# Sorting the second group's neighbour lists with one-hot matrix products inside layer 0, instead of through DRAM before it

## The chip, the core and the metric

The kernel runs on one core of a Trainium2 chip. The metric is the device time of one execution in microseconds (us). It ran three times before the change: 966.85, 970.43 and 974.26 us, so the median is 970.43 us. One further execution was profiled: it took 971.21 us, and its span from the first to the last instruction is 969.5 us.

## What is computed

The input is x with 3327 rows of 512 numbers, and a symmetric 0/1 matrix `adj` with about nine ones in a row. Two layers follow each other, each with a residual and a layer norm:

```
x = layernorm(x + relu(attention0(x, adj)))     # 4 heads of 128: softmax over the neighbours
x = layernorm(x + sigmoid(attn_a * x_a + attn_b * x_b))
    # x_a = weighted mean of h = x @ W_sa over the neighbours, x_b = adj @ (x @ W_g) + b
    # attn_a, attn_b = sigmoid of a sum over the neighbours of a scalar column
```

## The kernel before

The kernel is sparse. Row numbers are padded to 26 tiles of 128 nodes. It has three stages.

**Stage one (up to about 215 us).** For chunk after chunk of 512 nodes the adjacency is read, TensorE turns it into codes (line 379), and VectorE (DVE) extracts each node's neighbour numbers with repeated top-8 operations. The list of a node is a row of 32 words in `st`: its own number, 24 neighbour slots (S), its index in its group, and four words with its part of the attention logits. The nodes are in two groups, tiles 0 to 11 and tiles 12 to 25 (`NG`). Inside a group they are sorted by degree, so that a tile needs only as many slots as `CAPS` says. `rank_a` and `rank_b` (lines 454 to 485) give every node its place in the sorted order, `ranki`. `sort` (line 496) then moves the lists: one scatter per tile of 128 rows (helper at line 145) into the DRAM tensor `lists`, and one load (line 500) of the sorted lists into `srt`. For group 0 these steps are spread over stage one, between the stores of the feature rows to `table0` (line 361). For group 1 the rank is known only when the last chunk is decoded.

**Layer 0 (about 215 to 560 us).** Its loop (line 828) takes the 26 tiles in the hand-written order `order0`: tiles 11, 10, 0, 1, ..., 9 of group 0, then tile 23, tile 12 and the rest of group 1. Tiles 0 and 12 (`T0`) hold the nodes of the highest degree; their last slots are packed in a "staircase" that `climb` (line 542) prepares. In each iteration i, in program order:

- `gather` (line 592) for the tile three positions ahead (`AHEAD`): one indirect DMA per neighbour slot, issued by GpSimd (POOL), lines 609, 615 and 624, into a pool of seven buffers (`GB`) of six rows each;
- `publish` (line 793) of up to four finished tiles, after every fourth norm: ScalarE (ACT) scales them (line 795), and they are stored to `table1`;
- `columns2` (line 782): ACT copies the transposed rows of tile i-2 (line 784), TensorE (PE) multiplies them with eight columns (line 787);
- `attend` (line 748): for each slot DVE (line 760) or, for every third slot, ACT (line 758) weights the gathered row, and PE adds it up in PSUM with an identity product (bias at line 752, slots at line 763);
- for tile i-1: residual (line 843), transposes on PE (line 780), statistics, and at each fourth tile the inverse root (lines 669 to 676);
- `columns3` (line 790), in iteration 5 `climb(1)`, and `weigh_a`/`weigh_b` (lines 711, 738) of tile i+1: the logits (line 717), the exponential on ACT (line 730), and copies of the gathered node numbers into `srt` on ACT (line 734).

Each engine executes its instructions in the order in which they are written here; no scheduler reorders them.

The calls around the change stand ahead of the loop: the gathers of the first three tiles, then `sort(1)` with its 14 scatters on POOL and its load on SyncE's queue (SP), then two copies on SP (lines 811, 812) that build `own1`, a table of each group 1 node's x row beside its `table0` row. Group 1's gathers, from iteration 9 on, read `srt[1]` and `own1`.

**Layer 1 (about 560 us to the end).** The same gathers from `table1`, sums on DVE and PE, and two projections.

Of the kernel before, what the change touches and what calls it, by code (L numbers as in the profile page):

```python
# [8 lines left out]
F32 = mybir.dt.float32  # L9
AF = mybir.ActivationFunctionType  # L10
ALU = mybir.AluOpType
# [3 lines left out]
P = 128  # L15
LN_EPS = 1e-5
I32 = mybir.dt.int32
# [6 lines left out]
NG = (12, 14)  # L24
S = 24
# [4 lines left out]
LW = 32  # L30
# [49 lines left out]
def sparse_pass(  # L80
# [56 lines left out]
    dram = ctx.enter_context(tc.tile_pool(name="dram", bufs=1, space=bass.MemoryType.DRAM))  # L137
    table0 = dram.tile([NP, ROW], F32, name="table0")
    table1 = dram.tile([NP, ROW], F32, name="table1")
    own1 = dram.tile([NG[1] * P, 2, ROW], F32, name="own1")  # L140
    lists = [dram.tile([n * P, LW], I32, name=f"lists{i}") for i, n in enumerate(NG)]

    def scatter(group, dst, rows, src, last=None):

        put = nc.gpsimd.indirect_dma_start(  # L145
            out=dst, out_offset=bass.IndirectOffsetOnAxis(ap=rows, axis=0), in_=src, in_offset=None,
            bounds_check=last, oob_is_err=last is None,
        ).ins
# [8 lines left out]
    srt = [const.tile([P, n, LW], I32, name=f"srt{i}") for i, n in enumerate(NG)]  # L157
# [31 lines left out]
        return S + 1 if j in T0 else CAPS[j] + 1  # L189


    p0 = tc.alloc_tile_pool(name="p0", bufs=1, side="right")
    psl = tc.alloc_tile_pool(name="psl", bufs=1, space=PSUM, side="right")
    pj = tc.alloc_tile_pool(name="pj", bufs=1, side="left")
# [59 lines left out]
    for s in range(4):  # L254
# [5 lines left out]
        blk, pattern=[[P, 2]], base=0, channel_multiplier=1, allow_small_or_imprecise_dtypes=True  # L260
# [11 lines left out]
    )  # L272
    all1 = p0.tile([P, ND * NM], F32, name="all1")
    nc.gpsimd.memset(all1, 1.0)
    st = p0.tile([P, NT, LW], I32, name="st")
    nc.gpsimd.memset(st, 0)
    nc.gpsimd.iota(st[:, :, 0], pattern=[[P, NT]], base=0, channel_multiplier=1)
    for g, n in enumerate(NG):
        nc.gpsimd.iota(st[:, T0[g] : T0[g] + n, S + 1], pattern=[[P, n]], base=0, channel_multiplier=1)

    for s in range(2):
        for hh in range(2):
# [61 lines left out]
    def features(t):  # L344

        i = t * P // CH
        xc = xcs[i]
        o = t * P - chunks[i]
        pf = psf.tile([P, 2, 512], F32, tag="pf", name=f"pf{t}")
        for k, hh in ((k, hh) for hh in range(2) for k in range(KT)):  # L350
            nc.tensor.matmul(  # L351
                pf[:, hh, :HC], xc[:, k, o : o + P], w0[:, k, hh, :], start=(k == 0), stop=(k == KT - 1)
            )
        row = pj.tile([P, ROW], F32, tag="row", name=f"row{t}", bufs=4)
        nc.scalar.copy(row[:, 0:F].rearrange("p (h o) -> p h o", h=2), pf[:, :, 0 : F // 2])
        nc.scalar.activation(
            row[:, F : F + H], pf[:, 0, F // 2 : HC], AF.Identity, bias=pad if t == NT - 1 else 0.0
        )
        nc.scalar.copy(row[:, F + H : ROW], st[:, t, 0:1].to_broadcast([P, H]))
        nc.scalar.copy(st[:, t, S + 2 : S + 2 + H].bitcast(F32), pf[:, 1, F // 2 : HC])  # L360
        nc.gpsimd.dma_start(table0[t * P : (t + 1) * P, :], row)  # L361

    widths = [32 * ((len(ms) + 3) // 4) for ms in halves]
# [63 lines left out]
    def pick(i):  # L427

        t0, nt, g, l0 = span(i)
        nc.vector.tensor_reduce(ovf[:, t0 : t0 + nt, 0], codes_left[i][:, :nt], AX.X, ALU.max)  # L430
        nc.vector.tensor_scalar(ovf[:, t0 : t0 + nt, 1], ents[i][:, :nt, S - 1], -255.0, None, ALU.add)
        key = p0.tile([P, 4, S], F32, tag="key", name=f"key{i}")
        for j in range(nt):
            top8(nc, p0, key[:, j, :], cands[i][:, j].rearrange("p l s -> p (l s)"), LEVELS * S, "c", t0 + j)
        nc.vector.tensor_scalar(ovf[:, t0 : t0 + nt, 2], key[:, :nt, S - 1], -255.0, None, ALU.add)
        some = p0.tile([P, 4, S], F32, tag="some", name=f"some{i}")
        nc.vector.tensor_scalar(some[:, :nt], key[:, :nt], 255.5, None, ALU.is_gt)
        nc.vector.tensor_reduce(deg[g][:, l0 : l0 + nt], some[:, :nt], AX.X, ALU.add)
# [11 lines left out]
        nc.vector.tensor_scalar(st[:, t0 : t0 + nt, 1 : S + 1], some[:, :nt], float(N), None, ALU.add)  # L450

    hot = {}

# [10 lines left out]
    def rank_b(g):  # L464

        n = NG[g]
        w = ND * n
        oh = hot[g]
        tot = psl.tile([P, CH], F32, tag="pc0", name=f"tot{g}")
        nc.tensor.matmul(tot[:, :w], ones, oh, start=True, stop=True)  # L470
        pre = psl.tile([P, CH], F32, tag="pc1", name=f"pre{g}")
        nc.tensor.matmul(pre[:, :w], before, oh, start=True, stop=True)
        tots = p0.tile([P, ND * NM], F32, tag="tots", name=f"tots{g}")[:, :w]
        nc.vector.tensor_copy(tots, tot[:, :w])
        cum = p0.tile([P, ND * NM], F32, tag="cum", name=f"cum{g}")[:, :w]
# [9 lines left out]
        return ranki  # L485

    ranks = {}

# [2 lines left out]
    def later(n):  # L491
        for task in tasks[:n]:
            task()
        del tasks[:n]

    def sort(g, ranki, queue):

        put = lambda t: scatter(f"lists{g}", lists[g][:, :], ranki[:, t : t + 1], st[:, T0[g] + t, :])
        tasks.extend(lambda t=t: put(t) for t in range(NG[g]))
        tasks.append(lambda: queue.dma_start(srt[g], lists[g].rearrange("(t p) w -> p t w", p=P)))  # L500
        if g == 0:
            tasks.extend(lambda j=j: own_x(j) for j in range(NG[0]))
# [56 lines left out]
    for i in range(len(chunks)):  # L559
        make_codes(i)  # L560
        more(1)
        if i == NC0:
            rankis[0] = rank_b(0)
            sort(0, rankis[0], nc.gpsimd)
# [14 lines left out]
        more(4)  # L579
# [6 lines left out]


    gp = ctx.enter_context(tc.tile_pool(name="gp", bufs=1))
    m0 = ctx.enter_context(tc.tile_pool(name="m0", bufs=2))
    ps = ctx.enter_context(tc.tile_pool(name="ps", bufs=1, space=PSUM))  # L590

    def gather(table, j):
# [213 lines left out]
    AHEAD = 3  # L806
    for i in range(AHEAD):
        got[order0[i]] = gather(table0, order0[i])
    sort(1, rankis[1], nc.sync)
    later(len(tasks))  # L810
    nc.sync.dma_start(own1[:, 0, :], xo)
    nc.sync.dma_start(own1[:, 1, :], table0[NG[0] * P : NP, :])
    psl.release()
# [14 lines left out]
    for i in range(NT + 3):  # L828
# [21 lines left out]
                ]  # L850
        if 2 <= i < NT + 2:
            columns3(order0[i - 2])
        if i == 5:
            climb(1, m0, psx.tile([P, B * H], F32, tag="pcol", name="climb1", bufs=2)[:, : B + H])
        if i == NG[0]:
            nc.vector.memset(over, 0.0)
# [7 lines left out]
            weigh_b(order0[i + 1])  # L864
    covered()
    psx.release()


    w1 = ctx.enter_context(tc.tile_pool(name="w1", bufs=1, side="right"))
# [647 lines left out]
```

## Time and profile before

| | |
|---|---|
| runs | 966.85, 970.43, 974.26 us; median 970.43 |
| profiled execution | 971.21 us, span 969.5 us, mean granted TensorE clock 0.907 |
| busy | PE 804.4 us (83%), DVE 716.6 (74%), POOL 626.2 (65%), ACT 278.2 (29%) |
| chain that ended last | PE 45%, DVE 19%, DMA 12%, POOL 11%, issue 7%, ACT 4% |
| 180 to 215 us | PE busy 10.0 of 35, DVE 29.75, POOL 26.6 |
| 237 to 290 us | PE busy 47.4 of 53, DVE 32.3, POOL 40.5 |
| 420 to 500 us | PE busy 75.6 of 80, DVE 55.9, POOL 60.3 |

In a timeline, a row gives the start, the duration, engine, line and operation, output<-input and the count of instructions; in brackets the engine's idle time before it and what ended it. A float32 product appears as two MATMUL instructions. A POOL indirect DMA is about 0.96 us of work with 0.30 us to the next one, so 76% is what POOL shows when it issues without a pause.

### The profile page before, as it was taken

The numbers are of one execution on the slowest core, as the hardware profiler recorded it, in microseconds if no ns is written. First come the engines' busy times: TensorE is split into PE (matmuls) and PEld (weight loads), VectorE is DVE, ScalarE is ACT, GpSimd is POOL, SyncE is SP. The second block draws the span as 40 slices with busy tenths as digits, with TensorE's granted clock in tenths as the row PEclk, the third lists the DMA queues.
The fourth block names the chain that finished last, engine by engine and source line by source line (L and its number), as shares of the span: only waits on it lengthen the run. The fifth ranks groups of instructions, "written<-read, shape, count | busy, mean of one in ns | idle before, by whom it ended". The sixth has DMA issues, their size and how long they took to land.

```text
span 969.5 us, 10086 instructions
## 1 busy us (share of the span) xinstructions
PE 804.4 (83%) x2534; PEld 421.7 (43%) x2534; DVE 716.6 (74%) x2118; ACT 278.2 (29%) x820; POOL 626.2 (65%) x664
## 2 busy tenths in 40 slices
PE   4399887338897998989979839998989989899893
PEld 3277675114344444444434514444434434344341
DVE  4277878886465676667756738799989989989873
ACT  1022211004234343435333403223222232232231
POOL 6611144777777777677777367777777777777411
PEclk9699998557898999989998958999989999999997
DMA  9799999972988787787777257776676776666400
GB/s 321 289 353 376 399 332 382 360 205 76 401 312 247 218 271 225 257 282 231 231 227 232 92 166 192 195 187 188 189 197 196 187 195 183 187 185 188 129 33 36
DMA packets 74242, 221.87 MB, mean 229 GB/s; under 512 B 14944, under 2 KB 19216, under 8 KB 73280
## 3 DMA queue, kind: packets, MB, share of 16 engines
q0 software_dynamic: 47008, 153.87, 53.7%
q1 hardware_dynamic: 24512, 65.17, 17.7%
q10 hardware_dynamic: 2656, 2.10, 0.7%
q8 instruction: 23, 0.38, 0.2%
q14 instruction: 43, 0.35, 0.1%
HBM read 200.01 MB, written 28.55 MB: 236 GB/s over the span
## 4 chain that ended last, share of the span: by engine, by line
PE 45%; DVE 19%; DMA 12%; POOL 11%; issue 7%; ACT 4%; DVEq 0%; ACTq 0%; POOLq 0%
PE acc L763 21%; PE pf L351 9%; POOL g L615 7%; DMA g<-table,srt 7%; DVE sw L967 7%; DMA at<-in_adjB 3%; PE po L1007 3%; PE pcol L787 3%; PE acc L988 3%; PE acc L752 3%; DVE g L969 2%; ACT xt L784 1%; DMA a_row<-in_a_self 1%; PE x1t L780 1%; POOL sprod L321 1%
## 5 line engine op out<-in xcount | busy, mean ns | idle before, releaser
L615 POOL DMA_INDIRECT g<-table,srt x464 | 479.2, 1033 | 147.9 <-issue 121.9
L763 PE MATMUL acc<-g,ident 128*128 128x512 f32 x504 | 230.8, 614 | 1.4 <-DVE g L760 1.4
L967 DVE SCALAR_TENSOR_TENSOR sw<-g,e,sw 128x512 f32<-128x512 f32 x226 | 169.3, 749 | 12.7 <-ACT sw L951 8.5
L763 PEld LDWEIGHTS acc<-g,ident 128*128 128x128 f32 x504 | 100.4, 199 | 132.1 <-issue 101.1
L988 PE MATMUL acc<-g,ident 128*128 128x512 f32 x262 | 128.6, 618 | 24.9 <-DVE g L969 14.7
L351 PE MATMUL pf<-w,xc 128*128 128x260 f32 x416 | 102.2, 408 | 13.3 <-DVE w L291 13.3
L760 DVE TENSOR_TENSOR g<-g,w 128x512 f32<-128x512 f32 x176 | 110.5, 695 | 0.6
L1007 PE MATMUL po<-wg,sT 128*128 128x512 f32 x208 | 98.0, 616 | 0.0
L351 PEld LDWEIGHTS pf<-w,xc 128*128 128x128 f32 x416 | 83.6, 204 | 29.2 <-DVE w L291 14.1
L1007 PE MATMUL po<-wsa,sT 128*128 128x512 f32 x208 | 95.2, 601 | 0.3 <-ACT sT L1000 0.3
L758 ACT ACTIVATE g<-g,w 128x128 f32<-128x128 f32 x304 | 91.6, 389 | 0.7 <-DVE w L743 0.7
L988 PEld LDWEIGHTS acc<-g,ident 128*128 128x128 f32 x262 | 49.1, 193 | 95.8 <-issue 44.7
L361 POOL DMA_DIRECT2D table<-row x26 | 14.4, 555 | 85.4 <-ACT st L360 85.4
L969 DVE TENSOR_TENSOR g<-g 128x512 f32<-128x512 f32 x95 | 65.7, 692 | 3.3
L1037 ACT ACTIVATE za<-za 128x512 f32<-128x512 f32 x26 | 16.4, 631 | 170.8 <-DVE za L1035 170.8
L1007 PEld LDWEIGHTS po<-wg,sT 128*128 128x128 f32 x208 | 41.4, 200 | 52.2 <-issue 52.0
L1007 PEld LDWEIGHTS po<-wsa,sT 128*128 128x128 f32 x208 | 40.2, 194 | 51.3 <-issue 48.9
L145 POOL DMA_INDIRECT out<-za,srt x26 | 29.1, 1118 | 50.1 <-ACT za L1052 44.0
L787 PE MATMUL pcol<-v,xt 128*128 128x8 f32 x208 | 32.4, 283 | 33.1 <-ACT xt L784 33.1
L379 PE MATMUL pc<-at,pow 128*32 128x512 bf16 (+1 forms) x182 | 24.3, 436 | 33.2 <-DMA at<-in_adjB 19.4
L787 PEld LDWEIGHTS pcol<-v,xt 128*128 128x128 f32 x208 | 30.0, 222 | 38.8 <-ACT xt L784 38.6
L717 DVE TENSOR_TENSOR w<-g,srt 128x20 f32<-128x20 f32 (+3 forms) x55 | 9.7, 184 | 48.2 <-DMA g<-table,srt 46.9
(236 smaller groups left out, 933.3 us busy)
## 6 DMA issues: line engine op xcount, KB each, us to landing
at<-in_adjB SPq DMA_DIRECT2D x78, 512.0 KB, 11.4
g<-table,srt POOLq DMA_INDIRECT x464, 3.8
table<-row POOLq DMA_DIRECT2D x26, 260.0 KB, 6.2
xc<-in_xB SPq DMA_DIRECT2D x6, 1024.0 KB, 7.1
own<-in_xo SPq DMA_DIRECT2D x1, 3640.0 KB, 23.5
own<-table SPq DMA_DIRECT2D x1, 3640.0 KB, 42.0
at<-in_adjL SPq DMA_DIRECT2D x13, 256.0 KB, 13.2
table<-x1a SPq DMA_DIRECT2D x12, 260.0 KB, 5.7
```

The costliest lines, as they stand in the source:

```text
L145: put = nc.gpsimd.indirect_dma_start(out=dst, out_offset=bass.IndirectOffsetOnAxis(ap=rows, axis=0), in_=src, in_offset=None, bounds_check ...
L351: nc.tensor.matmul(pf[:, hh, :HC], xc[:, k, o : o + P], w0[:, k, hh, :], start=(k == 0), stop=(k == KT - 1))
L615: nc.gpsimd.indirect_dma_start(out=buf[:, q - q0, :], out_offset=None, in_=table[:, :], in_offset=bass.IndirectOffsetOnAxis(ap=srt[g][:, i ...
L752: nc.tensor.matmul(acc, ident, bias0, start=True, stop=False)
L758: nc.scalar.activation(gv[:, h, :], gv[:, h, :], AF.Copy, scale=w[:, s, h : h + 1])
L760: nc.vector.tensor_tensor(gv, gv, w[:, s, :].rearrange("p (h o) -> p h o", o=1).to_broadcast([P, H, FO]), ALU.mult)
L763: nc.tensor.matmul(acc, ident, buf[:, o + s - s0, 0:F], start=False, stop=(s == CAPS[j] and j not in T0))
L787: nc.tensor.matmul(pcol, xt1[:, k, :], v1[:, k, :], start=(k == 0), stop=(k == KT - 1))
L967: nc.vector.scalar_tensor_tensor(sw, g[:, i, 0:F], e[:, s : s + 1], sw, ALU.mult, ALU.add)
L969: nc.vector.tensor_add(g[:, i, 0:F], g[:, i - 1, 0:F], g[:, i, 0:F])
L988: nc.tensor.matmul(plain[j], to, row, start=(not sums_of_two and i == 0), stop=(sums_of_two and i == len(rows) - 1),)
L1007: nc.tensor.matmul(proj[j], sT[:, k, :], wt[:, k, :], start=(half + k == 0), stop=(half + k == KT))
```

## The change

- The lists of group 0 stay as they were (`st0`, `lists0`, `sort0`). The lists of group 1 are kept in float32 in `st1`, rows of 30 words, in a pool `ls` of its own. A small float32 tile `ids_f` holds the node numbers that `features` writes to `table0`.
- `rank_b(1)` also splits the place into tile and row, as float32 (`to`): four small DVE operations.
- `sort1` takes the place of `sort(1)`. For each of the 14 source tiles, DVE writes two operands, `row_is` (128x128: does this node go to that row?) and `spread` (128x420: the node's list in the columns of its destination tile, zeros elsewhere), each in two buffers. PE multiplies them and adds all 14 products up in one PSUM tile. Two source tiles are done in each of the iterations 1 to 7 of layer 0, after `columns3` and ahead of `weigh_a`. In iteration 7 DVE then copies the result to `srt[1]` in two parts.
- `climb(1)` moves from iteration 5 to iteration 8.
- The 14 scatters on POOL and the load on SP are gone; the `own1` copies on SP directly follow the last loads of the adjacency.
- The pool `m0` is released at the end of layer 0.

```diff
-    st = p0.tile([P, NT, LW], I32, name="st")
-    nc.gpsimd.memset(st, 0)
-    nc.gpsimd.iota(st[:, :, 0], pattern=[[P, NT]], base=0, channel_multiplier=1)
-    for g, n in enumerate(NG):
-        nc.gpsimd.iota(st[:, T0[g] : T0[g] + n, S + 1], pattern=[[P, n]], base=0, channel_multiplier=1)
+    st0 = p0.tile([P, NG[0], LW], I32, name="st0")
+    nc.gpsimd.memset(st0, 0)
...
+    st1 = ls.tile([P, NG[1], W1], F32, name="st1")
...
+    nc.gpsimd.iota(ids_f, pattern=[[P, NT]], base=0, **count)
...
+    columns = ls.tile([P, P], F32, name="columns")
+    nc.gpsimd.iota(columns, pattern=[[1, P]], base=0, **count)
+    tiles_ = ls.tile([P, NG[1], 1], F32, name="tiles_")
+    nc.gpsimd.iota(tiles_[:, :, 0], pattern=[[1, NG[1]]], base=0, **count)
...
+        ti = p0.tile([P, NM], I32, name="ti")
+        nc.vector.tensor_scalar(ti[:, :n], ranki[:, :n], 7, None, ALU.logical_shift_right)
+        nc.vector.tensor_scalar(ranki[:, :n], ranki[:, :n], P - 1, None, ALU.bitwise_and)
+        to = ls.tile([P, 2, NM], F32, name="to")
+        nc.vector.tensor_copy(to[:, 0, :n], ti[:, :n])
+        nc.vector.tensor_copy(to[:, 1, :n], ranki[:, :n])
...
+    def sort1(to, t0, t1):
+        n = NG[1]
+        if t0 == 0:
+            in_place.append(ps.tile([P, KT * P], F32, tag="pt", name="sorted1")[:, : n * W1])
+        for t in range(t0, t1):
+            row_is = ls.tile([P, P], F32, tag="row_is", name=f"row_is{t}", bufs=2)
+            nc.vector.tensor_scalar(row_is, columns, to[:, 1, t : t + 1], None, ALU.is_equal)
+            spread = ls.tile([P, n, W1], F32, tag="spread", name=f"spread{t}", bufs=2)
+            nc.vector.scalar_tensor_tensor(
+                spread, tiles_.to_broadcast([P, n, W1]), to[:, 0, t : t + 1],
+                st1[:, t : t + 1, :].to_broadcast([P, n, W1]), ALU.is_equal, ALU.mult,
+            )
+            nc.tensor.matmul(
+                in_place[0], row_is, spread.rearrange("p t w -> p (t w)"), start=(t == 0), stop=(t == n - 1)
+            )
+        if t1 == n:
+            by_tile = in_place[0].rearrange("p (t w) -> p t w", t=n)
+            nc.vector.tensor_copy(srt[1][:, :, : S + 2], by_tile[:, :, : S + 2])
+            nc.vector.tensor_copy(srt[1][:, :, S + 2 : W1].bitcast(F32), by_tile[:, :, S + 2 :])
...
-    sort(1, rankis[1], nc.sync)
-    later(len(tasks))
...
-        if i == 5:
+        if 0 < i <= 7:
+            sort1(rankis[1], 2 * i - 2, 2 * i)
+        if i == 8:
             climb(1, m0, psx.tile([P, B * H], F32, tag="pcol", name="climb1", bufs=2)[:, : B + H])
...
     psx.release()
+    m0.release()
```

More of the change, by code (lines that the diff above doesn't have):

```diff
@@ L140, in sparse_pass @@
     own1 = dram.tile([NG[1] * P, 2, ROW], F32, name="own1")
-    lists = [dram.tile([n * P, LW], I32, name=f"lists{i}") for i, n in enumerate(NG)]
+    lists0 = dram.tile([NG[0] * P, LW], I32, name="lists0")
     def scatter(group, dst, rows, src, last=None):
@@ L189, in slots @@
         return S + 1 if j in T0 else CAPS[j] + 1
+    ls = ctx.enter_context(tc.tile_pool(name="ls", bufs=1, side="right"))
     p0 = tc.alloc_tile_pool(name="p0", bufs=1, side="right")
@@ L274, in sparse_pass, with st @@
     nc.gpsimd.memset(all1, 1.0)
-    st = p0.tile([P, NT, LW], I32, name="st")
-    nc.gpsimd.memset(st, 0)
-    nc.gpsimd.iota(st[:, :, 0], pattern=[[P, NT]], base=0, channel_multiplier=1)
-    for g, n in enumerate(NG):
-        nc.gpsimd.iota(st[:, T0[g] : T0[g] + n, S + 1], pattern=[[P, n]], base=0, channel_multiplier=1)
+    st0 = p0.tile([P, NG[0], LW], I32, name="st0")
+    nc.gpsimd.memset(st0, 0)
+    nc.gpsimd.iota(st0[:, :, 0], pattern=[[P, NG[0]]], base=0, channel_multiplier=1)
+    nc.gpsimd.iota(st0[:, :, S + 1], pattern=[[P, NG[0]]], base=0, channel_multiplier=1)
+    count = dict(channel_multiplier=1, allow_small_or_imprecise_dtypes=True)
+    W1 = S + 2 + H
+    st1 = ls.tile([P, NG[1], W1], F32, name="st1")
+    nc.gpsimd.iota(st1[:, :, 0], pattern=[[P, NG[1]]], base=NG[0] * P, **count)
+    nc.gpsimd.iota(st1[:, :, S + 1], pattern=[[P, NG[1]]], base=0, **count)
+    ids_f = p0.tile([P, NT], F32, name="ids_f")
+    nc.gpsimd.iota(ids_f, pattern=[[P, NT]], base=0, **count)
+    count["channel_multiplier"] = 0
+    columns = ls.tile([P, P], F32, name="columns")
+    nc.gpsimd.iota(columns, pattern=[[1, P]], base=0, **count)
+    tiles_ = ls.tile([P, NG[1], 1], F32, name="tiles_")
+    nc.gpsimd.iota(tiles_[:, :, 0], pattern=[[1, NG[1]]], base=0, **count)
+    def st(t):
+        return (st0[:, t, :], st0[:, t, S + 2 : S + 2 + H].bitcast(F32)) if t < NG[0] else (
+            st1[:, t - NG[0], :], st1[:, t - NG[0], S + 2 : S + 2 + H]
+        )
     for s in range(2):
@@ L358, in features @@
         )
-        nc.scalar.copy(row[:, F + H : ROW], st[:, t, 0:1].to_broadcast([P, H]))
-        nc.scalar.copy(st[:, t, S + 2 : S + 2 + H].bitcast(F32), pf[:, 1, F // 2 : HC])
+        nc.scalar.copy(row[:, F + H : ROW], ids_f[:, t : t + 1].to_broadcast([P, H]))
+        nc.scalar.copy(st(t)[1], pf[:, 1, F // 2 : HC])
         nc.gpsimd.dma_start(table0[t * P : (t + 1) * P, :], row)
@@ L449, in pick @@
         )
-        nc.vector.tensor_scalar(st[:, t0 : t0 + nt, 1 : S + 1], some[:, :nt], float(N), None, ALU.add)
+        nc.vector.tensor_scalar(
+            (st0, st1)[g][:, l0 : l0 + nt, 1 : S + 1], some[:, :nt], float(N), None, ALU.add
+        )
     hot = {}
@@ L484, in rank_b @@
         ranks[g] = rk
-        return ranki
+        if g == 0:
+            return ranki
+        ti = p0.tile([P, NM], I32, name="ti")
[4 more added lines that the diff above has]
+        nc.vector.tensor_copy(to[:, 1, :n], ranki[:, :n])
+        return to
     ranks = {}
@@ L494, in later, with sort0 @@
         del tasks[:n]
[L496 to L502, printed above, removed]
+    def sort0(ranki):
+        put = lambda t: scatter("lists0", lists0[:, :], ranki[:, t : t + 1], st(t)[0])
+        tasks.extend(lambda t=t: put(t) for t in range(NG[0]))
+        tasks.append(lambda: nc.gpsimd.dma_start(srt[0], lists0.rearrange("(t p) w -> p t w", p=P)))
+        tasks.extend(lambda j=j: own_x(j) for j in range(NG[0]))
+    in_place = []
+    def sort1(to, t0, t1):
[9 more added lines that the diff above has]
+                st1[:, t : t + 1, :].to_broadcast([P, n, W1]), ALU.is_equal, ALU.mult,
+            )
+            nc.tensor.matmul(
+                in_place[0], row_is, spread.rearrange("p t w -> p (t w)"), start=(t == 0), stop=(t == n - 1)
+            )
+        if t1 == n:
+            by_tile = in_place[0].rearrange("p (t w) -> p t w", t=n)
+            nc.vector.tensor_copy(srt[1][:, :, : S + 2], by_tile[:, :, : S + 2])
+            nc.vector.tensor_copy(srt[1][:, :, S + 2 : W1].bitcast(F32), by_tile[:, :, S + 2 :])
     def own_x(j):
@@ L563, in sparse_pass @@
             rankis[0] = rank_b(0)
-            sort(0, rankis[0], nc.gpsimd)
+            sort0(rankis[0])
         turn_codes(i)
@@ L588, in sparse_pass @@
     gp = ctx.enter_context(tc.tile_pool(name="gp", bufs=1))
-    m0 = ctx.enter_context(tc.tile_pool(name="m0", bufs=2))
+    m0 = tc.alloc_tile_pool(name="m0", bufs=2, side="left")
     ps = ctx.enter_context(tc.tile_pool(name="ps", bufs=1, space=PSUM))
```

## The prediction, made before the changed kernel was run

> **What bounds the kernel now.** I read the 40 slices and the granted clock first, then the windows by stage, the chain of waits from 200 to 420 us, and the timelines of POOL, PE, DVE, ACT and SP there. The chain is mostly PE in layer 0 (acc L763 alone has 21% of the span). POOL shows where the change bites:
>
> ```profile
> 216.25 1.00 POOL L145 DMA_INDIRECT lists<-st,ranki  x1 [0.30 <-DVE w L729]
> ...
> 235.26 0.99 POOL L615 DMA_INDIRECT g<-table,srt  x1 [0.30 <-issue]
> ...
> 250.96 0.95 POOL L615 DMA_INDIRECT g<-table,srt  x1 [0.31 <-issue]
> ...
> 395.15 0.95 POOL L615 DMA_INDIRECT g<-table,srt  x1 [4.25 <-PE acc L763]
> ```
>
> The 14 scatters hold POOL from 216.25 to 235.26, 19.0 us. Behind them stand the 13 gathers of tile 1 (the loop's fourth); the last starts at 250.96 and lands at 257.25. POOL then issues without a pause until 390.9, where it waits 4.25 us for a buffer that layer 0's thirteenth iteration frees. So its 19 us of lag are worked off by then, and what the end feels of them is only the time that PE stood idle:
>
> ```profile
> 254.27 0.60 PE L780 MATMUL x1t<-ident,x1a 128*128 128x128 f32 x4
> 259.58 1.88 PE L787 MATMUL pcol<-v,xt 128*128 128x8 f32 x8 [4.71 <-ACT xt L784]
> 261.31 2.05 PE L752 MATMUL acc<-bias,ident 128*128 128x512 f32 x2
> 263.15 12.74 PE L763 MATMUL acc<-g,ident 128*128 128x512 f32 x26
> 275.73 0.60 PE L780 MATMUL x1t<-ident,x1a 128*128 128x128 f32 x4
> 277.06 1.06 PE L787 MATMUL pcol<-v,xt 128*128 128x8 f32 x8 [0.73 <-ACT xt L784]
> ...
> 302.28 0.29 PE L547 MATMUL climb<-of,to_row 128*128 128x14 f32 x2
> 308.33 1.87 PE L787 MATMUL pcol<-v,xt 128*128 128x8 f32 x8 [5.76 <-ACT xt L784]
> ```
>
> An ordinary iteration has one gap of 0.73 us: PE transposes, ACT copies (L784, 0.59), PE goes on. Two stand out: 4.71 us (the late gathers) and 5.76 us (iteration 5: DVE waits for PE's climb product, and `weigh_a` stands behind it). After both PE is slow for a while: pcol takes 1.88 and not 1.06, the bias 1.91 and not 0.96 (chain).
>
> ```profile
> 302.61 0.17 DVE L548 TENSOR_TENSOR of<-climb,step_of 128x10 f32<-128x10 f32 x1 [9.50 <-PE climb L547]
> ...
> 304.88 2.92 ACT L795 ACTIVATE x1a<-x1a,rdn,rrn 128x512 f32<-128x512 f32 x4
> 307.71 0.56 ACT L784 COPY xt<-x1t 128x512 f32<-128x512 f32 x1
> ```
>
> This is what it costs when DVE must wait for the end of PE's queue: its lead is gone. ACT's exponential waits for DVE, and behind the exponential, in ACT's order, stand publish and the copy that PE needs.
>
> ```profile
> 160.59 21.07 SPq L220 DMA_DIRECT2D at<-in_adjL  x13
> 236.49 0.39 SPq L500 DMA_DIRECT2D srt<-lists  x1
> 236.94 0.80 SPq L811 DMA_DIRECT2D own<-in_xo  x1
> 238.04 6.14 SPq L812 DMA_DIRECT2D own<-table  x1
> ```
>
> SP waited from 182 to 236 for the scatters; the own1 copies (3.64 MB each) followed.
>
> [...] the 2.51 us before to_rows at 386.7 also made the next 15 slots take 14.4 us where 12.9 is usual[...]. [...] the first own1 copy took 23.5 us to land, the second 42.0 from an issue 1.1 us later, one after the other.
>
> **The change part by part.** Iterations are i of layer 0.
>
> *Ahead of the loop.* Seven iotas and a smaller memset on POOL in place of three and a memset: the largest, 128x128, about 0.4 (the 128x350 one took 0.99). They lie in POOL's 6.29 us wait for a_row before 11.0; without that cover 0.3. Writing `st1` in float32 and reading `ids_f` cost what they replace. The four operations after the rank: 0.2 each from start to start (L483's kind), less DVE's 0.49 idle before L823: **+0.3**, on the path.
>
> *Products on PE.* A product of 512 columns takes 0.858 (24 instructions in 10.30 in the chain), so one of 420 takes 0.704, two 1.41, seven times **+9.9**. PE is the path here, so they count. In iterations 3, 4 and 6 they lie over the gap of 0.73, as ACT copies x1t meanwhile: **-2.2**.
>
> *DVE's operands.* row_is about 0.2 (L257, 128x128, 0.217), spread about 0.6 (L843, of its kind with 512 elements, 0.69): 1.6 an iteration. In 263 to 290 DVE is busy 19.45 of 27. Without its waits for gathers it leads PE by 6 to 10 us: in iteration 4 I get y at 271.5, statistics and inverse root to 275.1, operands to 276.8, weigh_a to 278, first weighted slot of iteration 5 at 279, where PE asks for it at 289. So **0**; if the lead were used up, 1.6 an iteration.
>
> *Scatters gone.* Tile 1's gathers: five from 216.25 into the free seventh buffer, five from 225.4 (tile 11's buffer, PE done at 225.1), three to 235.5; landed by 243 even with 8 us. DVE asks at 247.4. The later tiles' gathers wait for buffers and still land ahead of DVE (tile 2 by 258 for 260.3, tile 3 by 272 for 276.8, tile 4 by 284 for 289.5). The 4.71 us go, and the slow clock after them: 0.82 on pcol, 0.95 on the bias, 12.53 - 11.16 = 1.37 on the slots. **-7.85**.
>
> *Climb gone from iteration 5.* DVE does not wait, so ACT publishes (2.92) while PE still attends. The 5.76 us go, with 0.81 + 0.95 + 0.89 after them: **-8.4**. At this point, start of iteration 7's attend, PE is 9 to 10 us ahead of before.
>
> *New wait in iteration 7.* DVE's copies wait for the fourteenth product, which stands behind all of attend(7) and x1t. Queued behind them on DVE: weigh_a(8); behind that, on ACT: exponential, list copies, the copy for pcol. From the climb rows: copies 0.75 (L474, 350 elements from PSUM, 0.52; the second 0.18), weigh_a 1.15, exponential and list copies 0.65, ACT copy 0.6: 3.15, less 0.73: +2.4; slow clock 0 to 3.1, taken 2.3 (the 2.51 us gap cost 1.6, that of 3.39 us at 416.8 cost 3.0): **+4.7**.
>
> *Climb in iteration 8.* The same chain with 0.6 in place of the copies, 2.95, and 0.14 for the product, less 0.73; again 2.3: **+4.7**. The inverse root also falls in this iteration, 2.7 on DVE, but DVE needs 9 where PE needs 12. Publish in iteration 10 stays hidden.
>
> *own1 on SP at 182.* The last adjacency loads are used by PE until 193.1 and DVE needs the result at 195.5, 1.5 us after PE has it. [...] It then runs under the gathers of 190 to 235, as before under those of 237 to 280, where POOL kept its 1.26 us pace: **0**.
>
> *m0 released.* Layer 1's first ACT copy must wait for m0's last readers; it is at 557.6, the next ACT work at 573.9: 0.
>
> Sum: 0.3 + 9.9 - 2.2 - 7.85 - 8.4 + 4.7 + 4.7 = **+1.15**. From iteration 12 on all waits are on PE and DVE of the same loop (POOL is blocked by them at 391), so it shifts rigidly: span 970.65, execution 972.4. The profiled execution lies 0.8 above the median, so against the median 970.43 + 1.15 = **971.6**.
>
> **Rivals.**
>
> *POOL sets layer 0's pace, so all its relief reaches the end.* For it: its issue without a pause from 216 to 391. Against: PE busy 26.1 of 27 in 263 to 290, and the 4.25 us wait at 391. It would give 970.4 - 19 = 951. The milder form, where the two new waits in iterations 7 and 8 cost nothing, gives 962.
>
> *Slower: own1 collides with the last adjacency loads.* Seven loads are outstanding at 182; if own1 took equal turns with them, their 11 us would double, and DVE, whose work sets the path from 175 to 215, would start its last chunk up to 9.5 late: 981. It decides from a delay of 1.5 us on. [...]
>
> *Slower: DVE becomes the bound.* If spread, with two broadcast inputs, took twice 0.6, DVE would need 2.8 more an iteration; beyond its lead each iteration pays up to 1.6: 982. Against: L458, also with broadcast inputs, 350 elements in 0.52.
>
> *It does not do what it says: tile 1's gathers are held by buffers all the same.* Then the 7.85 stay: 979.5. Against: the buffer times above.
>
> **How the numbers follow.** Chances: forecast 0.65 (963 to 978: clock loss 0 to 3.1 twice is -4.6 to +1.6; products and operands -1 to +2; the runs before spread by 3.9), POOL's pace 0.10, own1 0.12, DVE 0.06, buffers 0.07. The range 962 to 982 leaves out most of the first rival and the tails. 1% is 9.7 us, about what a measurement here can tell: faster (below 960.7) 0.09 from the first rival, slower (above 980.1) 0.18 from half or more of the three slower ones and the forecast's tail, same 0.73.
>
> **What will show it.** No PE gap over 1 us in iterations 2 to 6; 14 products of about 0.7; two gaps near 3 us before pcol in iterations 8 and 9, each followed by a pcol of 1.9; POOL waiting on PE for buffers from 222 on; own1 landed by 240 and PE's first slot still near 218. A late first slot would mean own1; gaps filled by waits for DVE in every iteration, the DVE rival.

## The result, and the profile after

The changed kernel took 966.23 us (median of 20 runs, 963.85 to 972.38) against 970.38 us for the kernel before in the same sessions: ratio 0.9965, 95% interval 0.9952 to 0.9978. A second comparison on another chip gave 966.37 (22 runs) against 969.11 (47 runs), ratio 0.9974 (0.9958 to 0.9990). So the change saves 2.7 to 4.2 us. I had forecast 1.15 us more. The time lies inside the range, the sign of the likeliest case is wrong.

The profiled execution took 968.11 us, its span is 966.1 us, mean granted clock 0.910; busy PE 807.6 us, DVE 726.6, POOL 610.8 (15.4 less), ACT 278.9. Line numbers have moved: pcol is L839 (was 787), slots L815 (763). First the timeline of PE, around the pcol of iteration 3 and then of iterations 8 and 9 (columns: start, duration, engine, line and operation, output<-input; in brackets the idle time before it and what ended it):

```profile
258.52 1.58 PE L548 MATMUL sorted<-spread,row_is 128*128 128x420 f32 x4
259.94 0.95 PE L839 MATMUL pcol<-v,xt 128*128 128x8 f32 x8
...
324.60 1.58 PE L548 MATMUL sorted<-spread,row_is 128*128 128x420 f32 x4
328.89 1.06 PE L839 MATMUL pcol<-v,xt 128*128 128x8 f32 x8 [2.72 <-ACT xt L836]
...
340.61 0.29 PE L599 MATMUL climb<-of,to_row 128*128 128x14 f32 x2
343.78 1.19 PE L839 MATMUL pcol<-v,xt 128*128 128x8 f32 x8 [2.88 <-ACT xt L836]
344.82 2.06 PE L804 MATMUL acc<-bias,ident 128*128 128x512 f32 x2
```

This is the picture that I had drawn. The gap of 4.71 us in iteration 3 is gone, no row from 242 to 326 us shows PE idle, a pair of products takes 1.42 us from start to start, and the two new gaps are 2.72 and 2.88 us. DVE shows why they are there:

```profile
326.21 0.54 DVE L553 CAST srt<-sorted 128x364 int32<-128x364 f32 x1 [9.71 <-PE sorted L548]
...
340.94 0.17 DVE L600 TENSOR_TENSOR of<-climb,step_of 128x10 f32<-128x10 f32 x1 [3.87 <-PE climb L599]
```

The copies out of the product's buffer wait 9.71 us for PE, the climb's second half waits 3.87 us. POOL, which in the kernel before issued without a pause from 216 to 391 us, now waits for buffers (timeline of POOL, three of its rows with a long wait):

```profile
228.04 0.95 POOL L667 DMA_INDIRECT g<-table,srt  x1 [5.07 <-PE acc L815]
...
352.52 0.95 POOL L667 DMA_INDIRECT g<-table,srt  x1 [7.32 <-ACT x1a L847]
395.19 0.95 POOL L667 DMA_INDIRECT g<-table,srt  x1 [4.25 <-PE acc L815]
```

Most signs of the prediction's last section are there (the pcol behind the new gaps takes 1.06 and 1.19 us, not 1.9, and PE's first slot comes at 219.7, not 218), and yet the sum came out on the wrong side. One profile of each kernel does not tell where. By 561 us, where layer 1 starts, the changed kernel is 0.5 us *behind* (561.83 against 561.35). It passes the other in layer 1, whose code is the same, and after its last store:

```profile
core 0 of [0], span 969.5 us
960.57 0.98 POOL L145 DMA_INDIRECT out<-za,srt  x1 [2.07 <-ACT za L1052]
```

```profile
core 0 of [0], span 966.1 us
958.37 0.98 POOL L145 DMA_INDIRECT out<-za,srt  x1 [2.07 <-ACT za L1105]
```

From the last store's issue to the end of the span the kernel before needs 8.93 us, the changed one 7.73 us.

### The profile page after: what moved, and what is told of

It reads as the page before. It is cut to its first block, busy times and chain, and to the rows that moved or that the text cites. A ratio compares the mean times of both kernels' runs of the same rounds, so it can differ in the third digit from the quotient of the medians.

```text
span 966.1 us, 10166 instructions
## 1 busy us (share of the span) xinstructions
PE 807.6 (84%) x2562; PEld 424.7 (44%) x2562; DVE 726.6 (75%) x2152; ACT 278.9 (29%) x820; POOL 610.8 (63%) x654
## 4 chain that ended last, share of the span: by engine, by line
PE 38%; issue 20%; POOL 16%; DVE 11%; DMA 10%; ACT 3%; POOLq 0%; DVEq 0%; ACTq 0%
PE acc L815 21%; POOL g L667 10%; DMA g<-table,srt 8%; DVE sw L1020 5%; PE po L1060 5%; PE acc L1041 4%; PE pcol L839 3%; PE acc L804 3%; DVE g L1022 2%; DMA table<-row 1%; POOL table L379 1%; ACT xt L836 1%; PE x1t L832 1%; DMA a_row<-in_a_self 1%; POOL sprod L339 1%
## 5 line engine op out<-in xcount | busy, mean ns | idle before, releaser
L815 PE MATMUL acc<-g,ident 128*128 128x512 f32 x504 | 230.8, 614 | 1.6 <-DVE g L812 1.6
L1020 DVE SCALAR_TENSOR_TENSOR sw<-g,e,sw 128x512 f32<-128x512 f32 x226 | 169.5, 750 | 13.1 <-ACT sw L1004 8.9
L815 PEld LDWEIGHTS acc<-g,ident 128*128 128x128 f32 x504 | 100.1, 199 | 131.9 <-issue 99.4
L1060 PE MATMUL po<-wg,sT 128*128 128x512 f32 x208 | 95.5, 602 | 0.0
L145 POOL DMA_INDIRECT out<-za,srt x26 | 27.9, 1075 | 50.0 <-ACT za L1105 43.9
L839 PE MATMUL pcol<-v,xt 128*128 128x8 f32 x208 | 30.4, 273 | 25.5 <-ACT xt L836 25.4
L836 ACT COPY xt<-x1t 128x512 f32<-128x512 f32 x26 | 15.2, 584 | 97.3 <-PE x1t L832 97.3
L839 PEld LDWEIGHTS pcol<-v,xt 128*128 128x128 f32 x208 | 29.0, 213 | 32.0 <-ACT xt L836 30.9
## 6 DMA issues: line engine op xcount, KB each, us to landing
at<-in_adjL SPq DMA_DIRECT2D x13, 256.0 KB, 13.1
```

Source lines behind the costliest of these rows:

```text
L145: put = nc.gpsimd.indirect_dma_start(out=dst, out_offset=bass.IndirectOffsetOnAxis(ap=rows, axis=0), in_=src, in_offset=None, bounds_check ...
L815: nc.tensor.matmul(acc, ident, buf[:, o + s - s0, 0:F], start=False, stop=(s == CAPS[j] and j not in T0))
L839: nc.tensor.matmul(pcol, xt1[:, k, :], v1[:, k, :], start=(k == 0), stop=(k == KT - 1))
L1020: nc.vector.scalar_tensor_tensor(sw, g[:, i, 0:F], e[:, s : s + 1], sw, ALU.mult, ALU.add)
L1060: nc.tensor.matmul(proj[j], sT[:, k, :], wt[:, k, :], start=(half + k == 0), stop=(half + k == KT))
```

## The experiments

**The same kernels again.** No edit: the kernel before two more times, the changed kernel once.

> The kernel before, profiled a second time, for the spread of a profile. In the first profiles the changed kernel began layer 1 at 561.8 us against 561.4 and made its gain of 3.4 us only after that, 2.3 of it between 720 and 745 us. Theory A (the gain is made in layer 1 and belongs to the code): this profile has the same 5.99 us of po products and the same 3.21 us wait of the own_step instruction near 722 us, layer 1 lasts 408 us again, ratio to before 1.000. Theory B (the gain is made in layer 0 and one profile hid it): layer 1 starts 2 to 4 us later here than in a second profile of the changed kernel. Theory C (alignment that differs from execution to execution): the step at 722 us is missing here, and layer 1 lasts 405 to 406 us.

> The changed kernel, profiled a second time. Ratio 0.996 for all theories. Theory A (gain in layer 1, belongs to the code): layer 1 starts at 561 to 562 us and lasts 404 to 405 us, and the po products near 722 us take 3.7 us. Theory B (gain in layer 0): layer 1 starts at 557 to 559 us. Theory C (alignment by chance): the po products near 722 us take 6 us here, layer 1 lasts 407 us or more.

> The kernel before once more, for a third profile. In the first, layer 1 lasted 399.2 us to the last scatter, with a wait of 3.2 us behind half-speed products near 722 us, in the second 397.0 without it; five profiles of kernels with the change gave 396.0 to 397.1 and none had it. Theory 1 (the step comes and goes with the kernel before, by phase, and is worth about 1 us on the average): either value here, 397.0 or 399.2. Theory 2 (layer 1 is the same in both kernels): 397.0. Ahead of pcol in iteration 3, where I had put 4.7 us on the scatters, the wait was 4.7, 1.9 and 5.7 us with TensorE's first slot at 217.9, 222.5 and 220.5 us; it should lie in 1.8 to 6 us again.

Measured: ratios 1.0004 (0.9986 to 1.0022) for the kernel before against itself and 0.9974 for the changed one; before_third was executed once, 972.22 us. Here are the profiles, cut at four points, with three experiments that follow below; in them PE, DVE and ACT do the same work in layer 0 as in before or after:

| us | start of layer 0 | from there to the pcol of iteration 10 | rest of layer 0 | layer 1 to the last store | end |
|---|---|---|---|---|---|
| before | 214.4 | 142.0 | 205.0 | 399.2 | 8.93 |
| before_again | 219.0 | 136.2 | 205.2 | 397.0 | 8.89 |
| before_third | 215.9 | 143.0 | 205.6 | 397.1 | 8.92 |
| before_m0_freed | 217.0 | 143.2 | 205.6 | 397.0 | 8.93 |
| after | 216.0 | 140.3 | 205.5 | 396.5 | 7.73 |
| after_again | 215.3 | 138.1 | 206.1 | 396.7 | 7.75 |
| after_own1_late | 214.4 | 137.7 | 205.8 | 397.1 | 7.78 |
| after_14_more | 216.9 | 137.7 | 206.2 | 396.8 | 8.90 |

The start moves by 4.6 us in the kernel before alone, so the late start of the first profile after says nothing. Layer 1 is 399.2 in only one of the four profiles of before: most of what the first pair of profiles showed there was chance (Theory C of the first expectation). What is left is 2.6 us in the iterations up to the tenth (means 141.1 and 138.5; called iterations 0 to 10 from here on), 0.55 back in the rest of layer 0, 0.8 in layer 1 (0.3 without the one long profile) and 1.15 at the end. Only the end is the same in every profile of a kernel (the 8.90 us of after_14_more are explained below); the profiles of before spread over 7 us in iterations 0 to 10, so the 2.6 us are rough. The long column also shows that the kernel before differs from itself. In before_again, where layer 0 began 4.6 us later, the gap ahead of pcol in iteration 3 was not 4.71 but 1.85 us (PE):

```profile
261.78 1.06 PE L787 MATMUL pcol<-v,xt 128*128 128x8 f32 x8 [1.85 <-ACT xt L784]
```

POOL's scatters had begun only 2.8 us later than in the first profile (219.06 against 216.25), so the gathers behind them were less late for PE. In the other three profiles the scatters began 1.9 us after layer 0 and not 0.1, and this gap was 4.7, 4.9 and 5.7 us.

**m0 given up, alone.** The kernel before, with `m0` released after `covered()` as in the change.

> The kernel before with one part of the change alone: pool m0 is given up after layer 0, so that layer 1's pool m1 may lie where m0 was. Theory A1 (the other addresses of layer 1's buffers make the gain in layer 1): ratio 0.996 to 0.997, layer 1 about 3.4 us shorter than before's 408.2. Theory A2 (layer 1 gains because it starts in another phase against its gathers, not because of addresses): ratio 1.000, layer 1 408 us. A new wait at the start of layer 1 (m1 waits for m0's last reader) would show as a layer 1 that is 0.5 us or more longer.

Measured: 970.90 us, ratio 1.0007 (0.9993 to 1.0020); layer 1 397.0 us. Releasing the pool makes no gain.

**own1 later.** The changed kernel with

```diff
+        if i == 0:
+            nc.sync.dma_start(held, ws[order0[1]][:, 1, :])
+            nc.sync.dma_start(own1[:, 0, :], xo)
+            nc.sync.dma_start(own1[:, 1, :], table0[NG[0] * P : NP, :])
```

> The changed kernel with own1's two copies (3.64 MB each) held back on SP until the weights of the second tile are ready, near 222 us, by a small copy of those weights ahead of them; before had them at 237 us, the change at 184 us. Theory 1 (own1 delays the last adjacency loads): the tot product comes back to 208.4 us and TensorE's first slot to 217.9 us, 1.7 to 1.8 us earlier than in the changed kernel, and if later work shifts rigidly the ratio to before falls from 0.9965 to 0.9945 to 0.995. Theory 2 (the late start is chance, or the new index counts of the start make it): first slot stays at 219 to 220 us and the ratio at 0.9965. Own1 lands near 265 us, before tile 12's gather of it.

Measured: 966.50 us, against 966.37 for the changed kernel in the same session. The tot product came at 208.5 us, but with 208.4 to 213.1 us in the kernel before this is within what one kernel does. The copies at 184 us cost nothing that can be measured, as predicted. The last adjacency loads, issued from 174 us on, landed in 12.3 to 13.1 us with the copies behind them (first profile after) and in 12.6 to 12.7 us in the first profile of before. That own1 would start behind them was an assumption of the prediction; in which order the transfers moved was not shown.

**14 more indirect DMAs.** The changed kernel with, behind the last real gather of layer 1,

```diff
+        if i == NT - 1:
+            for k in range(14):
+                if k % U == 0:
+                    again = gp.tile([P, U, ROW], F32, tag="g", name=f"again{k}", bufs=GB)
+                nc.gpsimd.indirect_dma_start(
+                    out=again[:, k % U, :], out_offset=None, in_=table1[:, :],
+                    in_offset=bass.IndirectOffsetOnAxis(ap=srt[1][:, k, 1:2], axis=0),
+                )
```

> The changed kernel with 14 needless indirect gathers more on POOL after layer 1's last real gather; nothing reads them, and the output is unchanged. The end of the program, from the start of POOL's last scatter to the end of the span, takes 8.88 to 8.93 us in three profiles of the kernel before and 7.73 to 7.78 us in three of the changed one; in the trace's records it is GpSimd's closing drain, 7.16 against 6.01 us. Theory 1 (the drain grows with the number of indirect DMAs that the program issued, and 14 fewer give 1.15 us): the end takes 8.9 us again. Theory 2 (it depends on something else that the change altered, such as the buffers' addresses or the code's length): the end stays at 7.7 us. The ratio rises by 0.001 under Theory 1 if POOL's idle stretch of 12 to 28 us near the end hides the gathers themselves.

Measured: 968.33 us, ratio 0.9994 (0.9975 to 1.0012), a rise of 0.002 to 0.003 where 0.001 was expected, which the interval allows. The gathers ran from 910 to 929 us in POOL's idle time and held up nothing (layer 1 396.8 us). The end:

```profile
core 0 of [0], span 966.5 us
957.60 0.98 POOL L145 DMA_INDIRECT out<-za,srt  x1 [2.08 <-ACT za L1113]
```

8.90 us, the length of the kernel before; the closing drain of GpSimd in the trace's records is 7.16 us again. All fourteen profiles agree: with 560 indirect DMAs in the program the drain is 7.16 us, with 546 it is 6.01 or 6.02. So 1.15 us of the gain, 0.08 us for each indirect DMA less, are made after the work is done, and have to do with the number of such DMAs, not with where they stand.

**The two waits hidden.** The changed kernel with the copies and the climb's second half behind the next tile's weights:

```diff
-        if t1 == n:
-            by_tile = in_place[0].rearrange("p (t w) -> p t w", t=n)
...
-            climb(1, m0, psx.tile([P, B * H], F32, tag="pcol", name="climb1", bufs=2)[:, : B + H])
+            climbing = psx.tile([P, B * H], F32, tag="pcol", name="climb1", bufs=2)[:, : B + H]
+            climb_a(1, m0, climbing)
...
             weigh_a(order0[i + 1])
             weigh_b(order0[i + 1])
+        if i == 7:
+            sorted1()
+        if i == 8:
+            climb_b(1, m0, climbing)
```

`climb_a` is `climb` up to its product, `climb_b` the rest, `sorted1` the two copies.

> The changed kernel with the two waits of iterations 7 and 8 hidden: the two copies out of the product's buffer move behind the next tile's weights in iteration 7, and the climb is cut in two, its copies and product where they were in iteration 8, its VectorE part behind the next tile's weights. In three profiles of the changed kernel TensorE waits 2.7 and 2.9 us ahead of pcol there and iterations 8 to 10 take 8.7 us more than the same ones of before, of which 1.4 us is two products. Theory 1 (VectorE stands still behind a product of TensorE, and that wait is the cost): both gaps fall under 1 us and the time by 6 to 8 us, ratio to before 0.988 to 0.991. Theory 2 (POOL's gathers bind a few us behind TensorE): the gaps go but POOL's waits for buffers at 352 and 395 us shrink to nothing and the gain is 0 to 3 us, ratio 0.993 to 0.9965.

Measured: 957.52 us, ratio 0.9886 (0.9865 to 0.9906); iterations 0 to 10 take 129.6 us. Theory 1. PE around the pcol of iterations 8 and 9:

```profile
321.32 1.58 PE L548 MATMUL sorted<-spread,row_is 128*128 128x420 f32 x4
322.73 0.95 PE L849 MATMUL pcol<-v,xt 128*128 128x8 f32 x8
...
332.64 0.29 PE L606 MATMUL climb<-of,to_row 128*128 128x14 f32 x2
333.83 1.06 PE L849 MATMUL pcol<-v,xt 128*128 128x8 f32 x8 [0.90 <-ACT xt L846]
```

The difference is 138.5 - 129.6 = 8.9 us. Of it 8.1 us lie between the pcols of iterations 7 and 10, where the two waits and the slower PE after them are (42.3 us in the mean of the four profiles, 34.2 here; the granted clock in the first profile after was 0.83 from 330 to 340 us and 0.62 from 343.8 to 347.0 us); the other 0.8 lie ahead of them, where the two kernels are the same, so they are chance. I had put 9.4. This version beats both kernels, by 11.9 us and by 8 to 9, with not one instruction less.

**The products taken out.** The same kernel without the 14 products and their operands; part of the computation, the sort of group 1, is left out:

```diff
     def sort1(to, t0, t1):
+        return
...
-            by_tile = in_place[0].rearrange("p (t w) -> p t w", t=NG[1])
+            by_tile = st1
...
-        nc.vector.tensor_copy(flag, pb[0:1, 0:1])
+        nc.vector.tensor_scalar(flag, pb[0:1, 0:1], 0.0, None, ALU.mult)
```

> The changed kernel with the late reads, without the 14 products and their operands on VectorE: the second group's lists are copied as they stand, unsorted, and the flag for lists that are too long is held at zero, so that part of the computation (the sort of group 1) is left out. Theory 1 (my term: 14 products of 0.704 us less 2.2 us of filled waits, 7.7 us): iterations 2 to 8 take 7.7 us less than with the products, ratio near 0.981. Theory 2 (every iteration has a wait of 0.73 us ahead of pcol that the second product of a pair fills, so a pair costs 0.4 us as the spans of iterations 4 to 7 against the kernel with spread scatters say): 2 to 3 us less, ratio near 0.986.

Measured: iterations 0 to 10 take 127.3 us, 2.3 less than with the products. As a whole it took 960.53 us, ratio 0.9901: the rest of layer 0 is 4.1 us longer (210.2). DVE now waits there for gathers that have not landed, and PE for DVE:

```profile
370.39 0.18 DVE L767 TENSOR_TENSOR w<-g,srt 128x16 f32<-128x16 f32 x1 [3.54 <-DMA g<-table,srt]
```

So Theory 2 for the products, and a limit that neither theory had. The unsorted lists also make group 1's gathers fetch other rows; what that adds to the 4.1 us was not tried apart, so only the stretch up to iteration 10 is compared here. One iteration with products, then the same without, on PE:

```profile
296.51 0.60 PE L842 MATMUL x1t<-ident,x1a 128*128 128x128 f32 x4
296.95 1.58 PE L548 MATMUL sorted<-spread,row_is 128*128 128x420 f32 x4
298.36 0.95 PE L849 MATMUL pcol<-v,xt 128*128 128x8 f32 x8
```

```profile
295.53 0.60 PE L830 MATMUL x1t<-ident,x1a 128*128 128x128 f32 x4
296.86 1.06 PE L837 MATMUL pcol<-v,xt 128*128 128x8 f32 x8 [0.73 <-ACT xt L834]
```

From x1t to pcol PE needs 1.85 us with the products and 1.33 without. The pair costs 0.52 there, and the span from the pcol before to this one grows by 0.41 (13.04 against 12.63). So 1.0 of the pair's 1.41 us lies over time in which PE would have stood. The pairs of iterations 3 to 7 all add 0.41 or 0.42 in this way.

The pair of iteration 2 seems to save time: from the pcol of iteration 2 to that of iteration 3 it takes 19.14 us with the products and 20.14 without. The granted clock is what differs (0.91 and 0.83), and other profiles have it the other way round. These are four windows over the same stretch: this kernel with the products, without them, then the first profile of the changed kernel (with them), then the kernel with the scatters by four, which comes further down (without them). The columns are: window, its length, busy time and count for PE, PEld, DVE, ACT, POOL, then granted clock, DMA share, GB/s.

```profile
237.52:256.66 19.14, 19.14 (x52) 9.20 (x52) 18.30 (x41) 7.65 (x28) 12.85 (x13) 0.91 0.64 173
236.26:256.40 20.14, 19.47 (x47) 9.54 (x47) 17.24 (x37) 7.08 (x26) 13.49 (x14) 0.83 0.63 178
239.59:259.94 20.35, 20.35 (x52) 10.19 (x53) 19.05 (x42) 7.53 (x28) 13.08 (x13) 0.85 0.61 166
238.86:257.42 18.56, 17.89 (x48) 8.37 (x47) 17.04 (x37) 7.07 (x26) 14.69 (x13) 0.91 0.50 134
```

At a similar clock the products add 0.2 to 0.6 us here; the clock alone moves the stretch by 1.2 us with them (20.35 and 19.14) and by 1.6 without. So nothing shows that the products kept the clock up.

**The climb's wait hidden in the kernel before.** The same split of `climb`, at iteration 5 of the kernel before.

> The kernel before, with the climb of iteration 5 cut in two: its copies and product stay where they are, its VectorE part moves behind the next tile's weights. My term for the climb in the prediction was 8.4 us: a wait of 5.76 us and 2.65 us of slower TensorE after it. Theory 1 (the term stands, and the wait is VectorE standing behind the climb's product): the gap of 5.76 us ahead of pcol falls under 1.5 us, iterations 6 and 7 take 6 to 8.4 us less, ratio 0.991 to 0.994. Theory 2 (POOL holds the stretch up to 290 us and the rest): the gap is gone but a wait for gathers of the same length comes up within the next three iterations, ratio 0.998 to 1.000. Theory 3 (the lists' late landing is what is waited for): the gap stays at 4 us or more, as the product itself waits for the copies of the lists.

Measured: 968.15 us, ratio 0.9988 (0.9969 to 1.0007). The gap of 5.76 us is gone and iterations 0 to 10 shrink to 131.9 us, 9 less than the mean of before; but the rest of layer 0 grows to 211.6, 6 more. First PE behind the climb's product, then where the time was given back, ahead of tile 12:

```profile
300.34 0.29 PE L553 MATMUL climb<-of,to_row 128*128 128x14 f32 x2
301.24 1.06 PE L796 MATMUL pcol<-v,xt 128*128 128x8 f32 x8 [0.60 <-ACT xt L793]
...
381.23 0.65 PE L650 MATMUL to_nodes<-spread_n,to_node 128*128 128x40 f32 x2 [4.36 <-DVE spread_n L645]
```

```profile
379.60 0.18 DVE L726 TENSOR_TENSOR w<-g,srt 128x16 f32<-128x16 f32 x1 [4.99 <-DMA g<-table,srt]
...
393.17 0.95 POOL L624 DMA_INDIRECT g<-table,srt  x1 [2.45 <-DVE x1b L852]
```

PE waits for DVE and DVE for a gather: Theory 2, but at the end of iteration 12 and not within three of the climb's. POOL has no wait over 0.6 us from 216 us until the last row shown; with the 14 scatters in its queue it does not deliver tile 12 earlier.

**The scatters spread.** The kernel before with the lists' tiles in a pool of their own, `m0` released, own1 copied first, the climb split at iteration 8, and the scatters behind the gathers of an iteration in place of one train: in the first kernel two in each of iterations 1 to 7, in the second four in each of iterations 0 to 2 and the rest in iteration 3:

```diff
-    later(len(tasks))
...
             got[j] = gather(table0, j)
+        later(4)
```

> The kernel before with its 14 scatters of lists spread over iterations 1 to 7, two behind each iteration's gathers, the copy back in iteration 7 and the climb, cut in two as in the kernel before with the late climb, in iteration 8; the lists' tile and the ranks live in a pool of their own, m0 is given up as in the change, and own1 is copied at once on SP. So both waits of before are attacked and TensorE makes no sorted products. Theory 1 (the train of scatters ahead of tile 3's gathers was the cost, not the scatters): the gaps near 259 and 308 us fall under 1 us each, layer 0 becomes 14 to 16 us shorter than before's, ratio 0.984 to 0.986. Theory 2 (POOL is full: it is busy 106.8 us of the 140 us from 220 to 360, with 0.3 us lost at each of 110 instructions, together all of it): TensorE waits for gathers somewhere in iterations 3 to 9 for 8 us or more in all, ratio 0.992 to 1.000.

> The kernel before with its 14 scatters spread four behind the gathers of each of iterations 0 to 3 and the lists' copy back on SP behind the last, so that it no longer stands behind layer 1's first rows on SP and the climb's copies do not wait 20 us for it, as they did in the kernel with two scatters in each iteration; otherwise that kernel. Theory 1 (the scatters are free if they are spread): no gap over 1 us in iterations 2 to 9, layer 0 lasts 331 to 334 us, ratio 0.984 to 0.987. Theory 2 (POOL is full until tile 12, so the 14 scatters of 1.3 us each come back as late gathers): gaps of 8 us or more in all behind iteration 3, up to the gather of tile 12 near 380 us, layer 0 lasts 340 us or more, ratio 0.993 to 1.000.

Measured: 983.87 us, ratio 1.0150 (1.0127 to 1.0173), and 976.73 us, ratio 1.0055 (1.0033 to 1.0077). In the first the last scatter came at 349 us and the climb waited 20.3 us for the lists, which was the fault of my placing, so its time decides nothing. Its trace shows that from the pcol of iteration 2 to that of iteration 7, with eight scatters issued, PE has no wait over 0.73 us; what would have followed without the long wait is open. In the second no such thing is in the way, and PE waits here, DVE again for a gather:

```profile
303.51 0.18 DVE L727 TENSOR_TENSOR w<-g,srt 128x20 f32<-128x20 f32 x1 [6.18 <-DMA g<-table,srt]
...
308.40 1.87 PE L797 MATMUL pcol<-v,xt 128*128 128x8 f32 x8 [8.14 <-ACT xt L794]
...
391.80 0.65 PE L651 MATMUL to_nodes<-spread_n,to_node 128*128 128x40 f32 x2 [5.13 <-DVE spread_n L646]
```

Theory 2 again, and slower than its ratio of 0.993 to 1.000: 8.14 us ahead of the pcol of iteration 6 and 5.13 us at tile 12. By four or in one piece, the scatters' time on POOL comes back to PE. The train of the kernel before was the better of these orders; whether two in each iteration, with the lists in time for the climb, would be free was not run.

**One buffer.** The changed kernel with `bufs=1` for `row_is` and `spread`.

> The changed kernel with one buffer instead of two for each operand of the sorted products, row_is and spread. Theory 1 (two buffers let VectorE make both operand pairs of an iteration without waiting for TensorE, and without them VectorE stands behind the first product of every pair as it stands behind the last product in iteration 7): a gap of 2 to 3 us ahead of pcol in each of iterations 2 to 8, 14 to 22 us in all, ratio 1.010 to 1.020. Theory 2 (VectorE's wait is covered by the lead that it has over TensorE): gaps under 1 us, ratio 0.9965 to 0.998.

Measured: 994.85 us, ratio 1.0244 (1.0202 to 1.0287): Theory 1, though the time is more than its ratio and most of the gaps ahead of pcol are nearer 1 us. PE around the pcol of iteration 4, and DVE between the two products:

```profile
281.64 0.87 PE L548 MATMUL sorted<-spread,row_is 128*128 128x420 f32 x2
283.46 0.97 PE L548 MATMUL sorted<-spread,row_is 128*128 128x420 f32 x2 [0.95 <-DVE spread L544]
285.60 1.88 PE L839 MATMUL pcol<-v,xt 128*128 128x8 f32 x8 [1.17 <-ACT xt L836]
287.33 2.05 PE L804 MATMUL acc<-bias,ident 128*128 128x512 f32 x2
```

```profile
282.55 0.28 DVE L542 TENSOR_SCALAR row_is<-columns,to 128x128 f32<-128x128 f32 x1 [9.80 <-PE sorted L548]
```

DVE waits 9.80 us here for PE to read the one buffer, and `weigh_a` waits behind it. So it goes in each of the seven iterations, with waits of 5.6 to 9.8 us: the lead is lost seven times, not once. By the ratios (1.0244 against 0.9965 and 0.9974) the second buffer of each operand is worth about 27 us.

## Why the prediction was wrong

Against the first profile of before, which I had priced, my sum for layer 0 was -7.85 - 8.4 + 9.9 - 2.2 + 9.4 = +0.85; the changed kernel's mean gives 138.5 - 142.0 = -3.5. (Against the mean of four profiles of before, 141.1, it is -2.6.)

- *Scatters and climb gone, -7.85 and -8.4.* Right. The kernel without products and waits needs 127.3 where before needed 142.0: -14.7. My two terms, less the two ordinary gaps of 0.73 that stay in this kernel, make -14.8. That it is so close belongs to the profile that I priced: against the mean of four it would be -13.8. And they are one term, not two. The climb's wait alone, taken out of the kernel before, gave 1.2 us (interval -0.7 to 3.0); it pays because POOL lost its scatters at the same time. The scatters alone were not taken out. That the 19 us of lag "are worked off by then" was true only at the pace of the kernel before.
- *Products, +9.9 - 2.2.* **This step failed**, as the size of a term: it let too little of a pair lie over PE's wait. Counted as the comparison counts it (0.73 us covered in every pair but the first) my term is 9.9 - 4.4 = 5.5 us, and 2.3 were measured. The durations were right: a pair takes 1.41 us. But each of the pairs of iterations 3 to 7 hides 1.0 us and not 0.73, and so adds 0.41 and not 0.68: 0.73 is what the row shows, but from x1t to pcol there are 0.89 us without a start (1.33 less the 0.44 that back-to-back starts take), and pcol itself is 0.11 shorter directly behind a product. The pairs of iterations 1 and 2, for which I had 2.1 us, add nothing in this comparison (0.04), and that is in part luck of the clock: from layer 0's start to the pcol of iteration 3 it took 41.5 to 43.9 us in five profiles with two buffers and the products, and 40.8 to 41.4 in three kernels without the products and without the train of scatters ahead of tile 1. By these means all seven pairs cost about 3 us.
- *DVE's operands, 0.* Right with two buffers: no gap was added. With one buffer the kernel loses about 27 us.
- *Waits in iterations 7 and 8, +4.7 each.* Right in kind and place. Together they cost 8.1 to 8.9 us for 9.4 (10.1, if the 0.73 us of iteration 7 is counted with the products, as above). The slow clock did not come as priced: in the first profile pcol behind the first of them ran at 1.06 us, and the slots after it took 9.6 us in place of 7.9 (granted clock 0.83 from 330 to 340 us).
- *own1, 0, and m0, 0.* Right. Small operations ahead of the loop, +0.3: from pv1sum's product to PE's first slot it takes 5.38 us in place of 5.21, so +0.17.
- *From iteration 12 on it shifts rigidly.* Right to 0.55 us for layer 0 in this kernel, wrong for the end, a term that I had put at nothing: -1.15 us of closing drain. The drain stands in no row; the distance from the last row to the span, 8.93 us in the kernel before, shows where it is.

With the measured terms: -14.7 + 2.3 + 8.9 + 0.2 + 0.55 - 1.15 = -3.9, or -3.0 against the mean of before, and the timed differences are -4.15 and -2.7. The first three terms are differences of one or a few profiles, so this agreement is no finer than 1 to 2 us. Open is the rest in layer 1, 0.3 to 0.8 us in the means: the one profile with 399.2 us had a granted clock of 0.52 from 720 to 727 us, and eight po products took 5.99 us there, where 3.60 is usual. The kernel before with the climb's wait hidden, whose layer 1 is the same, had 398.7 us, and these products took 6.17 us; no profile of a kernel with the change had it, and whether the change made it rarer or that was chance is not shown.

Of the rivals, the mild form of "POOL sets the pace" (962 us, with waits that cost nothing) is nearest, and is half right. POOL's gathers held back what a saving on PE was worth in three runs (DVE waited 4.99 us for one with the climb's wait hidden in the kernel before, 6.18 with the scatters by four, 3.54 without the products); but the two waits were real, and 8 to 9 us were still to be had. How PE ran after a gap varied: gaps of 0.95 and 1.17 us within 4 us were followed by pcol at 1.88 and bias at 2.05 us (one buffer), and in the first profile after a single one of 2.88 us by a bias at 2.06. One of 2.72 us in the same profile was followed by pcol at 1.06 and bias at 1.11. So in this kernel a gap of 1 to 3 us is not priced by its length alone; the 2.3 us of slow clock that I put on each wait was my estimate from two gaps of one profile.

## What to carry to other kernels

Work put into PE's recurring wait cost only what stuck out of it here, 0.41 of a pair's 1.41 us: measure the wait from start to start, in every iteration, before pricing the work at its duration. A read of another engine's result belongs behind the work that this engine's lead depends on: moving two reads by a few lines gave 8 to 9 us here, at least twice what the change itself gave. And a gap that is closed on one engine can come back at the next supplier: without the climb's 5.76 us the kernel before gained 1.2 us (interval -0.7 to 3.0), and DVE waited 4.99 us for a gather ahead of tile 12; take out one gap alone and see whether the time stays out.

## What the runs showed of the hardware

- The end of the program grew with the number of indirect DMAs issued from POOL: 14 more, as scatters near 220 us or as gathers near 920 us, gave 1.15 us more in the closing drain (6.01 to 7.16 us), 0.08 us each. Two numbers of DMAs were run, 546 and 560.
- The granted clock of a stretch differs between executions of the same code, and can hide what an edit does: from the pcol of iteration 2 to that of iteration 3 the changed kernel took 20.35 us at 0.85 in one profile and 19.13 us at 0.91 in the next; without products two other kernels took 18.56 us at 0.91 and 20.14 us at 0.83.
- The same kernel's layer 0 started between 214.4 and 219.0 us. In the latest of them the wait for the gathers behind it was 1.85 us, in the other three 4.7 to 5.7, so one profile of a kernel prices such a gap badly.
- In iteration 5 of the kernel before, the rows of PE, DVE and ACT come in program order: ACT's copy (L784) of the transpose that PE began at 301.84 us started at 307.71 us, behind the exponential (L730, at 304.44 us, after a wait of 10.44 us for DVE) and publish (L795, at 304.88 us).
